# A four-layer graph network: its last two attention layers written as one run of steps

## The chip, the cores and the metric

The kernel runs on one core of a Trainium2 chip. The metric is the device time of one execution in microseconds. The kernel before takes 3355.96 us, the median of 3 runs (3355.28, 3355.96 and 3361.55).

An instruction belongs to one of five engines: TensorE (PE, matrix products; its weight loads are listed apart as PEld), VectorE (DVE), ScalarE (ACT), GpSimd (POOL) and SyncE (SP), which only issues loads. [...] Loads and stores are issued either on SP's queue or on GpSimd's.

## The reference, cut to what matters

Four layers follow one another on N = 2708 nodes of 512 features; each ends in a residual and a layer normalisation. The change touches the last two. `adj` is a 0/1 matrix with ones on the diagonal.

```python
# layer 2
node_att = softmax(x @ node_w, axis=0)
h = x @ edge_w
e = where(adj > 0, h @ h.T, -9e15)
edge_att = softmax(e, axis=1)
x = layernorm(x + (adj * (node_att * edge_att)) @ (x @ weight) + bias)
# layer 3
query, key, value = x @ Wq + bq, x @ Wk + bk, x @ Wv + bv
a = query @ key.T / sqrt(512) + adj + adj
x = layernorm(x + softmax(a, axis=-1) @ value)
```

## The kernel before, in words

**Blocks and groups.** The 2708 rows are cut into 22 blocks (`NT`, line 60): 21 of 128 rows and a last one, block 21, of 20 rows. Layers 2 and 3 treat the query rows in seven groups (`GROUPS`, line 975): six of three blocks, and a last one of blocks 18 to 21 (404 columns). A group's work is a row of 22 score steps, one for each block of keys, and 22 sum steps.

**A score step** (`one_score`, line 1086) loads the 128 x 384 piece of `adj` that belongs to it (`load_a`, five buffers, SP's queue), makes the scores in PSUM (`ps_s`, two banks), masks or biases them into a tile `e`, and takes a running maximum `mx`. Layer 2's scores are symmetric: those that have been made for an earlier group are read back from memory (`load_kept`) and transposed. After its 22nd score step a group spreads its maximum over the partitions (`spread_max`, line 1138). Block 21 has its own path: four partial products in quarters of a bank (L1112), a ScalarE copy, and one product that adds the quarters (L1122).

**A sum step** (`one_sum`, line 1174) subtracts the maximum and takes the exponential, adds to the denominator `acc`, in layer 2 multiplies by `adj` (L1382, with a load of its own), and multiplies by the values (L1195): `sup` in layer 2, `xs` itself in layer 3, where the weight `wv` is applied to the finished sum. Block 21's values come from `values4`, four copies of its 20 rows that GpSimd's queue loads when the layer begins (L1055).

**The end of a group** (`end`, line 1233) takes the denominators (L1245), and puts the work on single blocks into a list `later`. In layer 2 that is `finish2` (line 1384): residual sum (L1388), layer normalisation, and a transpose of the new rows into `hT` (L1003 and L1006), which is then layer 3's key. In layer 3 it is a projection by `wv` (L1273) and `finish3` (line 1438): GpSimd adds bias and residual into `y` (two buffers, L1441), VectorE adds the sum (L1442) and normalises, and GpSimd's queue stores the block (L1446).

**The order.** A loop at line 1290 makes one score step and the sum step that lies `lag` = 25 steps behind, so a layer is 154 + 25 = 179 steps: 25 with scores alone, then 129 with both, then 25 with sums alone. At odd steps of a group one entry of `later` is run; what is left runs after the loop. A scheduler then places each engine's instructions within this order by when they should be ready, so neighbours may be interleaved.

**The two layers** are two calls of `softmax_layer`. Each call opens its own pools of buffers and closes them at its end; between the calls `sup` is freed, and layer 3's weights are loaded into space opened for them: the query weight in four pieces (L1417), `wv` (L1418) and `bv` (L1419). Layer 3's first step makes the query of group 0 (line 1420, products L1013).

Of the kernel before, what the change touches and what calls it, by code (L numbers as in the profile page):

```python
# [29 lines left out]
def gnn_stack_kernel(  # L30
# [991 lines left out]
    def softmax_layer(keys, values, query, score, weigh, finish, after=None, mirror=False):  # L1022
# [5 lines left out]
        AHEAD = 3  # L1028
        HOME = {it: gi for gi, group in enumerate(GROUPS) for it in group}

        def key_order(gi):

            late = list(range(NFULL // 2)) + [NT - 1] + list(range(NFULL // 2, NFULL))
            if not mirror:
                return late
            early = [jt for jt in late if HOME[jt] < gi]
            late = [jt for jt in late if HOME[jt] >= gi]
            place = {jt: (k + 0.5) / len(early) for k, jt in enumerate(early)}
            place |= {jt: (k + 0.5) / len(late) for k, jt in enumerate(late)}
            return sorted(place, key=place.get)  # L1040
# [6 lines left out]
        with (  # L1047
            tc.tile_pool(name="att", bufs=2) as att,
            tc.tile_pool(name="att_ps", bufs=2, space=PSUM) as psum,
        ):  # L1050


            values4 = att.tile([P, F], F32, tag="values4", name="values4", bufs=1)
            for c in range(C):
                nc.gpsimd.dma_start(values4[c * Q : c * Q + REST], values[:REST, NT - 1, :])  # L1055

            def load_a(gi, jt):
                c0, w = GSPAN[gi]
                j0, m = BLOCKS[jt]
                a = att.tile([P, GW], F32, tag="a", name="a_cols", bufs=5)  # L1060
                if m < P:
                    nc.vector.memset(a, 0.0)
                for r in range(0, P, P if m == P else Q):
                    nc.sync.dma_start(a[r : r + m, :w], adjT[j0 : j0 + m, c0 : c0 + w])
                return a

            def load_kept(gi, jt):

                g = HOME[jt]
                src = kept[g, gi][:, j_in(jt)]  # L1070
                s = att.tile([P, GB, P], F32, tag="sm", name="s_kept", bufs=3)
                full = sum(BLOCKS[it][1] == P for it in GROUPS[gi])
                nc.sync.dma_start(
                    s[:, :full, :], src[: full * P].rearrange("(b p) j -> p b j", p=P)
                )
                for b in range(full, len(GROUPS[gi])):
                    n = BLOCKS[GROUPS[gi][b]][1]
                    nc.sync.dma_start(s[:n, b, :], src[b * P : b * P + n])
                return s

            def j_in(jt):

                b = jt - GROUPS[HOME[jt]][0]
                return slice(b * P, b * P + BLOCKS[jt][1])

            def one_score(st, k):
                gi, jt = st["gi"], st["order"][k]
                c0, w = GSPAN[gi]
                j0, m = BLOCKS[jt]
                a = load_a(gi, jt)  # L1090
                ps = psum.tile([P, BANK], F32, tag="ps_s", name="ps_s")
                if mirror and HOME[jt] < gi:
                    s = load_kept(gi, jt)
                    for b, it in enumerate(GROUPS[gi]):
                        n = BLOCKS[it][1]
                        nc.tensor.transpose(
                            ps[:, b * P : b * P + n], s[:n, b, :], ident[:n, :n]
                        )
                elif m == P:
                    for c in range(C):  # L1100
                        nc.tensor.matmul(  # L1101
                            ps[:, :w],
                            keys[:, c, j0 : j0 + P],
                            st["q"][:, c, :],
                            start=(c == 0),
                            stop=(c == C - 1),
                        )
                else:

                    parts = psum.tile([P, BANK], F32, tag="tp", name="ps_parts")  # L1110
                    for c in range(C):
                        nc.tensor.matmul(  # L1112
                            parts[c * Q : (c + 1) * Q, :w],
                            keys[:, c, j0 : j0 + Q],
                            st["q"][:, c, :],
                            start=True,
                            stop=True,
                        )
                e = att.tile([P, GW], F32, tag="e", name="e", bufs=NT + AHEAD + 2)
                if m < P:  # L1120
                    nc.scalar.copy(e[:, :w], parts[:, :w])
                    nc.tensor.matmul(ps[:, :w], quarters, e[:, :w], start=True, stop=True)  # L1122
                if mirror and HOME[jt] > gi:
                    s = att.tile([P, GROUP * P], F32, tag="sraw", name="s_raw", bufs=3)
                    nc.scalar.copy(s[:m, :w], ps[:m, :w])
                    nc.gpsimd.dma_start(kept[gi, HOME[jt]][j_in(jt), :], s[:m, :w])
                score(e[:, :w], ps[:, :w], a[:, :w])
                st["e"].append(e)
                if k == 1:
                    st["mx"] = att.tile([P, GW], F32, tag="mx", name="mx", bufs=1)  # L1130
                    nc.vector.tensor_tensor(
                        st["mx"][:, :w], st["e"][0][:, :w], e[:, :w], ALU.max
                    )
                elif k > 1:
                    mx = st["mx"][:m, :w]
                    nc.vector.tensor_tensor(mx, mx, e[:m, :w], ALU.max)

            def spread_max(st):

                gi = st["gi"]  # L1140
                c0, w = GSPAN[gi]
                k = len(GROUPS[gi])
                tp = psum.tile([P, C, P], F32, tag="tp", name="tp_mx")
                nm = small.tile([P, GB], F32, tag="nm", name="nm")
                dg = att.tile([P, GB, P], F32, tag="dg", name="dg", bufs=1)
                for b, it in enumerate(GROUPS[gi]):
                    n = BLOCKS[it][1]
                    nc.tensor.transpose(
                        tp[:n, b, :], st["mx"][:, b * P : b * P + n], ident
                    )  # L1150
                    nc.vector.tensor_reduce(
                        nm[:n, b : b + 1], tp[:n, b, :], AX.X, ALU.max, negate=True
                    )
                    nc.vector.tensor_scalar(
                        dg[:n, b, :n], ident[:n, :n], nm[:n, b : b + 1], None, ALU.mult
                    )
                pb = psum.tile([P, BANK], F32, tag="tp", name="pb")
                full = sum(BLOCKS[it][1] == P for it in GROUPS[gi])
                nc.tensor.matmul(  # L1159
                    pb[:, : full * P],  # L1160
                    ones,
                    dg[:, :full, :].rearrange("p b i -> p (b i)"),
                    start=True,
                    stop=True,
                )
                for b in range(full, k):
                    n = BLOCKS[GROUPS[gi][b]][1]
                    nc.tensor.matmul(
                        pb[:, b * P : b * P + n], ones[:n], dg[:n, b, :n], start=True, stop=True
                    )  # L1170
                st["nmax"] = att.tile([P, GW], F32, tag="nmax", name="nmax", bufs=2)
                nc.scalar.copy(st["nmax"][:, :w], pb[:, :w])  # L1172

            def one_sum(st, k):
                gi, jt = st["gi"], st["order"][k]
                c0, w = GSPAN[gi]
                j0, m = BLOCKS[jt]
                e = st["e"][k][:, :w]
                nc.vector.tensor_tensor(e, e, st["nmax"][:, :w], ALU.add)
                nc.scalar.activation(e, e, AF.Exp)  # L1180
                if k == 0:
                    st["acc"] = att.tile([P, GW], F32, tag="acc", name="acc", bufs=1)
                    nc.vector.tensor_copy(st["acc"][:, :w], e)
                    st["po"] = [
                        psum.tile([P, F], F32, tag=f"po{(GROUP * gi + b) % C}", name="po", bufs=1)
                        for b in range(C if after is not None else len(GROUPS[gi]))
                    ]
                else:
# [118 lines left out]
            for work in later:  # L1307
                work()
# [211 lines left out]
```

## Time and profile before

| What | Value |
|---|---|
| median of 3 runs | 3355.96 us |
| profiled execution | 3363.59 us |
| its span, first to last instruction | 3361.8 us |
| mean granted TensorE clock | 0.985 of full |
| PE busy | 3272.6 us (97%) |
| VectorE, ScalarE, GpSimd busy | 1991.5, 1344.1, 130.0 us |
| first score product of layer 2 / of layer 3 | 1697.4 / 2410.2 us |
| last product of a sum in layer 2 / in layer 3 | 2387.5 / 3336.2 us |

Times are in us from the first instruction. A row of a timeline gives start, length, engine, line, operation, what it writes and reads by the program's own names, shape and count, and in brackets how long the engine was idle before it and what released it. PE's ends are modelled, since products overlap. Line numbers are those of the kernel before. A float32 product is made in two passes, so a score step of four products shows eight instructions.

### The profile page before, as it was taken

The page shows a single profiled execution, that of the slowest core. Times are in us where ns is not written, and L with a number is a line of the kernel's source. Part 1 is how long each engine was busy: PE and PEld are TensorE (multiplying, and loading weights), DVE is VectorE, ACT ScalarE, POOL GpSimd, SP SyncE. Part 2 cuts the span into 40 slices and gives each one's busy share as a digit, 9 for nine tenths or more (in the row PEclk, how much of TensorE's full clock was granted, in tenths as well). Part 3 has the DMA queues.
Part 4 walks back from the last instruction along what each step waited for, and adds up shares of the span by engine and source line. Part 5 has one row for each costly group of instructions (what it writes and reads, how often), then busy time and mean ns, then how long its engine had stood idle before and what let it go on. Part 6 is the DMA issues. An engine that isn't in the chain of part 4 may idle for free.

```text
span 3361.8 us, 30553 instructions
## 1 busy us (share of the span) xinstructions
PE 3272.6 (97%) x10981; PEld 1751.3 (52%) x10981; DVE 1991.5 (59%) x3228; ACT 1344.1 (40%) x1504; POOL 130.0 (4%) x211
## 2 busy tenths in 40 slices
PE   8999999999999989999999999999999999999998
PEld 5444444544444445886554554444455555555554
DVE  7878967767687585445135666777253442543533
ACT  6888887468877652001133333332011010110110
POOL 1000100000000000000010000000000000000001
PEclk9999999999999999999999999999999999999999
DMA  8746753335534412540044444554211111111100
GB/s 292 249 159 199 274 185 104 112 106 181 183 131 159 157 40 75 140 128 15 0 119 131 118 123 130 141 149 109 63 49 35 44 33 42 37 34 44 35 23 20
DMA packets 168348, 367.32 MB, mean 109 GB/s; under 512 B 20782, under 2 KB 111602, under 8 KB 164804
## 3 DMA queue, kind: packets, MB, share of 16 engines
q1 hardware_dynamic: 153268, 301.55, 30.0%
q0 software_dynamic: 14928, 63.82, 5.0%
q8 instruction: 86, 1.41, 0.2%
q14 instruction: 66, 0.54, 0.1%
HBM read 301.46 MB, written 63.35 MB: 109 GB/s over the span
## 4 chain that ended last, share of the span: by engine, by line
PE 73%; issue 13%; DVE 7%; DMA 3%; ACT 3%; POOL 1%; SPq 0%; POOLq 0%; DVEq 0%; ACTq 0%
PE po L1195 22%; PE ps_s L1101 17%; PE po L397 8%; PE ps_nb L952 7%; PE ps_wide L1013 4%; DVE t L349 3%; PE ps_hid L118 2%; PE ps_sup L1338 2%; PE ps_o L1273 2%; PE ps_mlp L637 2%; DMA a<-adj_d 1%; ACT t L341 1%; DMA a_cols<-in_adjT_dram 1%; PE ps_dec L733 1%; ACT t L350 1%
## 5 line engine op out<-in xcount | busy, mean ns | idle before, releaser
L349 DVE SCALAR_TENSOR_TENSOR t<-t,a 128x2708 f32<-128x2708 f32 (+1 forms) x162 | 480.0, 2974 | 146.6 <-ACT t L341 144.8
L341 ACT ACTIVATE t<-f1b,f2h 128x1354 f32<-128x1354 f32 (+1 forms) x324 | 445.7, 1414 | 93.2 <-PE psm L420 45.1
L397 PE MATMUL po<-t,emb 128*128 128x452 f32 (+3 forms) x1056 | 408.3, 556 | 17.9 <-ACT t L350 10.1
L350 ACT ACTIVATE t<-t 128x2708 f32<-128x2708 f32 (+1 forms) x162 | 396.7, 2452 | 70.3 <-DVE t L349 68.9
L397 PE MATMUL po<-t,xw 128*128 128x452 f32 (+3 forms) x1056 | 415.8, 557 | 9.0 <-ACT ft L499 4.8
L1195 PE MATMUL po<-sup,e 128*128 128x512 f32 x882 | 409.3, 600 | 5.5 <-DVE e L1382 5.5
L1195 PE MATMUL po<-e,xs 128*128 128x384 f32 (+1 forms) x1176 | 407.5, 489 | 0.0
L1101 PE MATMUL ps_s<-q,hT 128*128 128x384 f32 (+1 forms) x1176 | 403.5, 489 | 0.0
L1436 DVE SCALAR_TENSOR_TENSOR e<-a_cols,ps_s 128x384 f32<-128x384 f32 (+1 forms) x154 | 85.6, 556 | 417.3 <-PE ps_s L1101 394.2
L397 PEld LDWEIGHTS po<-t,emb 128*128 128x128 f32 (+1 forms) x1056 | 197.2, 194 | 222.3 <-issue 197.3
L1101 PEld LDWEIGHTS ps_s<-q,hT 128*128 128x128 f32 x1176 | 222.7, 190 | 161.4 <-issue 6.5
L397 PEld LDWEIGHTS po<-t,xw 128*128 128x128 f32 (+1 forms) x1056 | 191.0, 192 | 221.0 <-issue 202.5
L1195 PEld LDWEIGHTS po<-e,xs 128*128 128x128 f32 x1176 | 221.7, 190 | 157.1 <-issue 6.0
L1195 PEld LDWEIGHTS po<-sup,e 128*128 128x128 f32 x882 | 161.8, 191 | 176.5 <-issue 148.4
L1101 PE MATMUL ps_s<-hT 128*128 128x384 f32 (+1 forms) x672 | 229.2, 488 | 1.0 <-ACT sup L1345 0.7
L98 ACT ACTIVATE ln_rstd<-ln_rstd 128x1 f32<-128x1 f32 x88 | 17.2, 201 | 497.5 <-DVE ln_rstd L97 497.0
L1378 ACT ACTIVATE a_cols<-a_cols,neg_big 128x384 f32<-128x384 f32 (+1 forms) x154 | 94.8, 616 | 251.6 <-DMA a_cols<-in_adjT_dram 222.9
L952 PE MATMUL ps_nb<-hid_hi,at 128*128 128x512 f32 x484 | 188.2, 390 | 0.4 <-DVE at L946 0.4
L952 PE MATMUL ps_nb<-hid_lo,at 128*128 128x512 f32 x484 | 187.9, 390 | 0.0
L1172 ACT COPY nmax<-pb 128x384 f32<-128x384 f32 (+1 forms) x14 | 6.7, 478 | 431.2 <-PE pb L1159 350.4
L1101 PEld LDWEIGHTS ps_s<-hT 128*128 128x128 f32 x672 | 125.9, 190 | 97.0 <-issue 19.0
L1190 DVE TENSOR_TENSOR acc<-acc,e 128x384 f32<-128x384 f32 (+2 forms) x294 | 162.6, 553 | 11.2 <-ACT e L1180 1.0
(234 smaller groups left out, 3486.0 us busy)
## 6 DMA issues: line engine op xcount, KB each, us to landing
a<-adj_d SPq DMA_DIRECT2D x116, 677.0 KB
a_cols<-in_adjT_dram SPq DMA_DIRECT2D x378, 192.0 KB
a<-in_adjT_dram SPq DMA_DIRECT2D x42, 677.0 KB
adj_d<-a POOLq DMA_DIRECT2D x42, 677.0 KB, 4.7
raw<-in_adjT_dram SPq DMA_DIRECT2D x105, 256.0 KB
kept<-t POOLq DMA_DIRECT2D x10, 1354.0 KB, 6.4
t<-kept SPq DMA_DIRECT2D x10, 1354.0 KB
a_cols<-in_adjT_dram SPq DMA_DIRECT2D x63, 202.0 KB
```

What stands on the lines that cost most here:

```text
L118: nc.tensor.matmul(ps[:n], xt[:, c, :n], w[:, c, :], start=(c == 0), stop=(c == C - 1))
L341: nc.scalar.activation(tv[:, k, :], f1b[:n, k, :w], AF.Tanh, bias=f2h[:n, jt, h : h + 1], scale=0.5,)
L349: nc.vector.scalar_tensor_tensor(tv, tv, GUARD, ab, ALU.add, ALU.mult)
L350: nc.scalar.activation(tv, tv, AF.Exp, scale=0.5)
L397: nc.tensor.matmul(po[HB * k + q][:, :qw], values[r : r + n, jt, h * P : (h + 1) * P], t[r : r + n, k, q0 : q0 + qw], start=(jt == 0), sto ...
L952: nc.tensor.matmul(pos[it], at, half[:, jt, :], start=(jt == 0 and k == 0), stop=(jt == NT - 1 and k == 1),)
L1013: nc.tensor.matmul(ps[:, :width], w(c, o), xt(c), start=(c == 0), stop=(c == C - 1),)
L1101: nc.tensor.matmul(ps[:, :w], keys[:, c, j0 : j0 + P], st["q"][:, c, :], start=(c == 0), stop=(c == C - 1),)
L1190: nc.vector.tensor_tensor(acc, acc, e[:m], ALU.add)
L1195: nc.tensor.matmul(out, lhsT, rhs, start=(k == 0), stop=(k == NT - 1))
L1378: nc.scalar.activation(a, a, AF.Identity, bias=neg_big[: a.shape[0]], scale=1.0e30)
L1436: nc.vector.scalar_tensor_tensor(e, a, 2.0, ps, ALU.mult, ALU.add)
```

## The change

`softmax_layer` no longer opens pools or loops. It takes the pools and the list `later`, and gives back two functions, one that makes a score step and one that makes a sum step. Both layers share one set of pools, and one loop runs both: 345 steps in place of 179 + 179. Layer 3's query of group 0 and its score steps begin at step 166, while layer 2's sums go on to step 178; its sums begin at step 191.

- Layer 3's tiles that had space of their own now lie in `sup`, in blocks whose last use in layer 2 has gone by: queries in blocks 0 to 7, `wv` in 8 to 11, `bv` in 12, the finished sums in 13 to 16, and `y` in 17 to 20, so that four places take turns instead of two.
- The query weight is loaded at step 154 into buffers that layer 2's stored scores used (three in `sm`, the last quarter in two of `sraw`); `wv` and `bv` are loaded at step 179. All are on SP's queue.
- `values4` is loaded at a layer's first sum step instead of its first step.
- Group 0 of layer 3 takes the key blocks in the order 0 to 21, with block 21 last; the other groups have block 21 in the middle as before.
- Entries of `later` run at odd steps as before, and also at every step that has no sum: layer 2's last four blocks are finished at steps 179 to 182.
- The stores of the last group's four blocks go on SP's queue; those of the other groups stay on GpSimd's.

The diff, cut to its core (the body of the step functions is only indented otherwise):

```diff
+    def softmax_layer(
+        att, psum, later, keys, values, query, score, weigh, finish, after=None, sums=None
+    ):
...
             if not mirror:
-                return late
+                return late if gi else list(range(NT))
...
-            values4 = att.tile([P, F], F32, tag="values4", name="values4", bufs=1)
-            for c in range(C):
-                nc.gpsimd.dma_start(values4[c * Q : c * Q + REST], values[:REST, NT - 1, :])
+        def last_values():
+
+            t = att.tile([P, F], F32, tag="values4", name="values4", bufs=1)
             for c in range(C):
+                nc.gpsimd.dma_start(t[c * Q : c * Q + REST], values[:REST, NT - 1, :])
+            values4.append(t)
...
-                    oT = att.tile([P, C, GW], F32, tag="oT", name="oT", bufs=1)
+                oT = sums()
...
-            later = []
-            states = {}
-            steps = len(GROUPS) * NT
-            lag = NT + AHEAD
-            for t in range(steps + lag):
-                if t < steps:
-                    gi, k = divmod(t, NT)
-                    if k == 0:
-                        states[gi] = {
-                            "gi": gi, "e": [], "q": query(gi, att, psum), "order": key_order(gi)
-                        }
-                    one_score(states[gi], k)
-                    if k == NT - 1:
-                        spread_max(states[gi])
-                if t >= lag:
-                    gi, k = divmod(t - lag, NT)
-                    one_sum(states[gi], k)
-                    if k == NT - 1:
-                        end(states.pop(gi))
-                    elif later and k % 2:
-                        later.pop(0)()
-            for work in later:
-                work()
+        def score_step(t):
+            gi, k = divmod(t, NT)
+            if k == 0:
+                states[gi] = {"gi": gi, "e": [], "q": query(gi), "order": key_order(gi)}
+            one_score(states[gi], k)
+            if k == NT - 1:
+                spread_max(states[gi])
+
+        def sum_step(t):
+            gi, k = divmod(t, NT)
+            if t == 0:
+                last_values()
+            one_sum(states[gi], k)
+            if k == NT - 1:
+                end(states.pop(gi))
+
+        return score_step, sum_step
...
+        def weights3():
+
+            mqk = []
+            for o in range(C):
+                if o + 1 < C:
+                    t = att.tile([P, GB, P], F32, tag="sm", name=f"mqk{o}", bufs=3)
+                    nc.sync.dma_start(t[:, :C, :], mqk_d[o])
...
+        def values3():
+            wv_sb = room(8, 4, C, F)
+            nc.sync.dma_start(wv_sb, wv.rearrange("(c p) o -> p c o", p=P))
+            bv_sb = room(12, 1, F)
+            nc.sync.dma_start(bv_sb, bv.partition_broadcast(P))
...
+        def query(gi):
             c0, w = GSPAN[gi]
-            q = att.tile([P, C, GW], F32, tag="q", name="q")
+            q = room(4 * (gi % 2), 4, C, GW)
...
-            y = att.tile([P, F], F32, tag="y", name="y3")
+            y = room(17 + it % 4, 1, F)
...
-                nc.gpsimd.dma_start(out[i0 : i0 + n, :], y[:n])
+                queue = nc.sync if it in GROUPS[-1] else nc.gpsimd
+                queue.dma_start(out[i0 : i0 + n, :], y[:n])
...
+        steps = len(GROUPS) * NT
+        lag = NT + AHEAD
+        start3 = steps + 12
+        assert start3 + GROUPS[-1][0] >= steps + lag + GB
+        for t in range(start3 + steps + lag):
+            if t == steps:
+                weights3()
+            if t == steps + lag:
+                values3()
+            if t < steps:
+                score2(t)
+            elif 0 <= t - start3 < steps:
+                score3(t - start3)
+            k = None
+            for first, step in ((lag, sum2), (start3 + lag, sum3)):
+                if 0 <= t - first < steps:
+                    step(t - first)
+                    k = (t - first) % NT
+            if later and (k is None or (k % 2 and k < NT - 1)):
+                later.pop(0)()
+        for work in later:
+            work()
```

`room(first, blocks, *shape)` is a view of `blocks` blocks of `sup` from block `first` on.

## The prediction

> **What bounds the kernel now.** I read the table of stretches first, cutting the run at the layer boundary and at the end. Columns: length, then busy time (and instructions) of TensorE (PE), its weight loads, VectorE (DVE), ScalarE (ACT), GpSimd (POOL); then granted PE clock, DMA share, GB/s.
>
> ```profile
> 2330.00:2389.85 59.85, 59.84 (x175) 23.57 (x173) 21.68 (x50) 10.70 (x18) 0.00 (x0) 1.00 0.17 42
> 2389.85:2399.76 9.91, 3.26 (x17) 2.61 (x17) 7.67 (x26) 2.74 (x9) 1.40 (x2) 0.66 0.93 329
> 2399.76:2483.00 83.24, 79.84 (x247) 46.01 (x247) 35.84 (x72) 11.80 (x23) 3.27 (x5) 0.98 0.21 54
> 2483.00:3280.00 797.00, 796.96 (x2508) 453.36 (x2507) 336.48 (x699) 97.85 (x209) 27.21 (x30) 1.00 0.14 37
> 3336.70:3361.80 25.10, 14.77 (x41) 5.82 (x39) 11.50 (x29) 0.81 (x4) 4.63 (x6) 0.86 0.09 33
> ```
>
> Layer 2's last sums keep PE busy 59.84 of 59.85 us, and layer 3's body 796.96 of 797. A change of order can gain nothing there: the same matmuls remain. What can be gained lies in rows two and five, and 3.4 us in row three.
>
> The timeline of PE shows what row two consists of (start, length; idle time before and its releaser in brackets), under a steady example from layer 2:
>
> ```profile
> 2340.51 0.60 PE L1003 MATMUL tp<-ident,xs 128*128 128x128 f32 x4
> ...
> 2396.05 3.26 PE L1003 MATMUL tp<-ident,xs 128*128 128x128 f32 x16 [6.21 <-DVE xs L113]
> 2399.76 10.59 PE L1013 MATMUL ps_wide<-hT,mqk 128*128 128x384 f32 x32 [0.45 <-ACT hT L1006]
> ```
>
> After the last product, four blocks are finished on VectorE while TensorE waits 6.21 us; the 16 transposes then take 3.26 us, another 0.45 us goes by, and only then does layer 3's first query start. In the chain of waits a steady set of four transposes takes 0.44 us, so 16 are worth 1.76.
>
> Last, the end. The timeline of VectorE and GpSimd, and the rows of the closing line:
>
> ```profile
> 3350.93 1.26 POOL L1441 TENSOR_TENSOR y<-xs,bv_sb 20x512 f32<-20x512 f32 x1 [1.81 <-DMA out_dram<-y]
> 3352.22 0.74 DVE L1442 SCALAR_TENSOR_TENSOR y<-ps_o,rs,y 20x512 f32<-20x512 f32 x1 [1.15 <-POOL y L1441]
> 3355.34 0.52 POOL L1446 DMA_DIRECT2D out_dram<-y  x1 [2.66 <-DVE y L113]
> ...
> L1516 POOLq DRAIN x3: 46/99/5683, 3355.3 to 3361.5; - x3
> L1516 SPq DRAIN x3: 7/7/7, 3357.7 to 3361.3; - x3
> L1516 PEldq DRAIN x2: 13/3058/6103, 3345.4 to 3361.3; - x2
> ```
>
> PE is done at 3345.4 + 6.1 = 3351.5, yet the last block's sum starts at 3352.22, because GpSimd's addition into y had to wait for a store to free one of two y buffers. SyncE (SP), which waits for every store, passes at 3357.7. GpSimd's DRAIN begins as its last store is issued, at 3355.3, and takes 5.68 us, to 3361.0; the closing barrier ends the span 0.8 us later. GpSimd's drain sets the end, not the landing.
>
> **The boundary.** The change puts layer 3's query and scores 0 to 12 beside layer 2's last 13 sum steps. A score step costs PE 2.58 us (32 matmuls in 10.32 us, four steps), one of these sum steps (10.50 + 1.00) / 4 = 2.87. Side by side they make 5.45 per step, no less than one after the other: nothing is gained in the overlap itself. The gain is row two: when the last sum ends, scores 13 to 17 are ready to run, 5 × 2.58 = 12.9 us that need no late block. At best 9.91 − 1.76 = 8.15 us goes.
>
> What is late next? VectorE must close four blocks and serve those scores. From 2389.00 it took 7.0 us to the first transpose; two or three scores in that time add 1.1 us each (scores' e and running maximum, 0.55 + 0.56), so some 10 us if shared. PE's cover is 0.9 us of small matmuls plus 12.9, so score 18, the first that needs a late block, is not late. The order of instructions can still hurt: the program lists the first transposes right after score 13, which PE reaches at 0.9 + 2.6 = 3.5 us, while that block's chain alone (first three sums 2.5, score 13's two operations 1.1, the fourth sum 0.9, normalisation 2.2) takes 6.7: 3.2 us of idle PE. But the other 18 blocks of layer 2 are listed in the same way, each behind its own normalisation, and the waits list has 7.3 us for this wait in all, 6.2 of it here: 1.1 us over the rest. Instructions are plainly interleaved with ready work (the steady transposes stand between products). Bounds of what remains: 0 and 4.9 (below); I take 0.8, nearest to the steady rows. **Gain 7.3 us.**
>
> A rule bears on the upper bound. Row: after 6.21 us idle the clock granted from 2392 to 2398 is 0.50 to 0.52, and the transposes need 0.21 us each instead of 0.11; after 3.93 us idle at a group's end (2317) it is 0.53 for 3 us; after layer 3's broken idle at 2468 (1.24 us at most in one piece) row three still has 0.98. The Trainium skill, "TensorE: Matmul & The Clock Gate", Part 1, halves the clock after an idle window of about 3.4 us and asks as much busy time to restore it; the window runs freely. By the rule a remaining 3.2 us wait can cost half of 3.4 us more, 1.7, so 4.9; by the rows a wait near 1 us costs only itself. I go by the rows for the value, by the rule for the bound. The rule also says that the saved clock loss is no extra gain: it is already inside the 3.26.
>
> **Hidden parts of the move.** The overlapped steps ask VectorE for five operations, 2.8 us, of 5.45, and the loads for two tiles per step, as in all of layer 2: nothing. Layer 3's first set of sums has its usual lag. Its group 0 now takes block 21 last, not in the middle: its 0.60 us wait for the ScalarE copy moves and keeps its price, and the 2.8 us of idle at the first spread of the maximum (1.24 + 0.39 + 0.38 + 0.80) stay, since no sums run there. So row three's 3.4 us is not gained.
>
> **Loads.** Five query-weight loads now stand in SP's queue at the last score of layer 2, and wait there until the transposes of blocks 15 to 17 free their buffers, at 2304.1 on the old clock; loads for layer 2's sums are queued behind. Issue: 5 × 0.43 = 2.2 us. The cover: SP's last load before the group's end was issued at 2304.94, the next at 2320.86, as VectorE needs nothing new before 2320. Cost nothing; without that cover, 2 us of issue plus 3 us for 1 MB at 329 GB/s. wv (1 MB) and bv stand before score 13's loads: 3 us against five loaded tiles ahead, 5 × 2.58: nothing. GpSimd's four small loads of the last value rows move from each layer's start to its first sum: 4 × 0.51 us, used ten or more steps later: nothing; their lateness would cost at most their 4.3 us.
>
> **The end.** With four y places, block 21's addition runs early, after block 17's store lands (issued 3298.2 + 2.6). Its sum then starts at 3351.55 instead of 3352.22, 0.7 us sooner, and its normalisation (2.8 us) ends at 3354.35. The store goes by SP. No store on SP is in the trace: its landing is bounded by the 1.9 us of 40 KB loads on GpSimd's queue and the 2.6 us median of 256 KB stores; below, 1.5, if the 0.5 us issue there is mostly saved. I take 1.9, same size: 3356.3, and with 0.8 for the barrier 3357.1, against 3361.8: 4.7, of which I count 4.6 (3.9 to 5.1). GpSimd's drain now begins near 3303, 48 us of cover for its 5.7; with that cover gone the gain would be the 0.7.
>
> Here two rules speak against so much. "DMA: Bandwidth & Descriptors", Specifications, has a first byte at 1 us by GpSimd and 0.6 by SP: 0.4 gained. "VectorE: DVE Perf Modes", The DRAIN you can't avoid, calls the drains at a program's ends about 12 ns on all engines: then no drain is saved, and 0.7 + 0.4 = 1.1 is all. The row has 5683 ns. I go by the row. **Gain 4.6 us.**
>
> **Sum.** 7.3 + 4.6 = 11.9 us. Span 3361.8 → 3349.9; the profiled execution, 3363.59, would become 3351.7. It lies 7.6 us above the median of the runs, which I take off alike: 3355.96 − 11.9 = 3344.1.
>
> **Rivals.**
> - *Both gains as summed*: 3344.1, own range 3341 to 3347. Chance 0.64.
> - *The wait moves into the transposes*: 3.2 us idle behind score 13 plus 1.7 of clock; the boundary gives 3.2, total 7.8: 3348.2. For it: VectorE is nearly full for 10 us. Against: 1.1 us over 18 blocks. Chance 0.21.
> - *The overlap doesn't happen* (layer 3's query or scores wait for something of layer 2's last sums): only the end gains, 3351.4. For it: query results go into the space of values still in use. Against: the query's four blocks are read in the first eight steps of that group, before it starts. Chance 0.10.
> - *Slower: one big tile, ordered as a whole.* Queries, sums, weights and outputs of layer 3 all lie in sup. If accesses to one tile were ordered whatever part they touch, each output block's chain (3344.59 to 3347.5, 2.9 us) would stand before the next score that reads the query. 18 blocks × 2.9 = 52 us: 3396. It decides from 11.9 / 2.9, over four such waits. Against: hT is one tile also, ScalarE writes its blocks while scores read others, and the list of waits has no score waiting for that. Chance 0.05.
>
> **The numbers.** A measurement can tell about 0.2% from no change, 6.7 us: faster means below 3349.2. The first case is; of the second about 0.16, by the spread of its bounds; the third is "same" with the rest. Faster 0.80, same 0.15, slower 0.05. Low end: both gains in full, 13.2 us, and 0.1% for the medians (the three runs before span 6.3 us): 3339.5. High end: the second case and 2 us: 3350.5; the last two are left out, 0.15.
>
> **What would show it.** Right: no PE idle over 1 us at the boundary, transposes in fours between scores at 0.11 us each, clock 1.0 throughout; SP's last store near 3354 on the old clock less 7, GpSimd's drain long before. Wrong: a wait for DVE xs before the first transposes with the clock at 0.5; a long GpSimd drain at the end still; PE waits in the body of layer 3, now 0.04 us; or loads late in the overlapped steps.

## The result and the profile after

The changed kernel takes 3348.45 us, the median of 9 runs (3344.59 to 3354.89), against 3359.08 for the kernel before in 9 runs (3355.28 to 3366.54). The ratio is 0.9969, 95% interval 0.9961 to 0.9978: some 10.4 us (7 to 13) faster. The forecast was a gain of 11.9 us, to 3344.1 us; of the 4.3 us between that and 3348.45, 3.1 lie in the kernel before, which took 3355.96 us in the first 3 runs and 3359.08 in all 9.

The profiled spans differ by more, 3361.8 to 3346.3, and 4.0 us of that is no effect of the change: layer 2's first score product starts at 1697.45 before and at 1693.43 after, though nothing ahead of it was edited. In the traces of this study that start lies anywhere from 1692.7 to 1700.2 (1693.2 in the kernel before with one line moved at its very end). So the two traces, and all experiments, are compared from there on, in two pieces:

| Piece | before | after | difference | forecast |
|---|---|---|---|---|
| first score product of layer 2 to last sum product of layer 3 ("the middle") | 1638.8 | 1631.6 | -7.2 | -7.3 |
| last sum product to the end of the span ("the end piece") | 25.6 | 21.3 | -4.3 | -4.6 |

A single trace can carry such differences: kernels whose instructions up to the last sum product are the same have middles of 1638.8 and 1639.0 us (the kernel before, twice) and of 1631.6, 1631.6 and 1631.7 (the changed kernel, three times). The end piece with the stores on SP's queue varies more, from 20.9 to 21.5 us.

**The boundary.** The table of stretches of the changed kernel, in the columns of before, cut in the overlapped steps, around the end of layer 2's last sum, around layer 3's first spread of the maximum, and in the body of layer 3:

```profile
2363.00:2425.00 62.00, 62.00 (x184) 30.34 (x183) 18.70 (x32) 0.00 (x0) 3.75 (x3) 1.00 0.30 86
2425.00:2445.00 20.00, 20.00 (x77) 10.88 (x76) 13.57 (x43) 4.43 (x10) 3.50 (x5) 1.00 0.21 52
2445.00:2470.00 25.00, 21.51 (x65) 11.55 (x64) 15.20 (x34) 8.13 (x17) 0.00 (x0) 0.86 0.16 42
2470.00:3270.00 800.00, 799.96 (x2517) 454.93 (x2517) 338.21 (x707) 100.08 (x213) 27.64 (x30) 1.00 0.14 36
```

The second row is the boundary: TensorE is busy for 20.00 of 20.00 us at full clock, where it had been idle for 6.66. The timeline of TensorE shows by what:

```profile
2427.71 0.97 PE L1252 MATMUL pr<-ones,acc 128*128 128x1 f32 x8
2428.61 0.91 PE L1108 MATMUL ps_s<-sup,hT 128*128 128x384 f32 x2
2429.45 1.03 PE L1268 MATMUL ps_po<-po,quarters 128*20 128x512 f32 x2
2430.41 8.01 PE L1108 MATMUL ps_s<-sup,hT 128*128 128x384 f32 x24
2438.26 0.60 PE L1003 MATMUL tp<-ident,xs 128*128 128x128 f32 x4
```

The closing of the last group (pr, ps_po) is followed at once by scores (ps_s), 26 passes of them, a little more than three score steps, before the first transposes. Those come after 9.6 us, when VectorE has closed the first block, and no bracket shows a wait. They were not put right behind score 13, as the program lists them.

**The end.** The timeline of VectorE and SP, and the rows of the closing line (durations in ns, least, median and most, then the first and the last start):

```profile
3332.85 10.64 SPq L1484 DMA_DIRECT2D out_dram<-sup  x4
3340.33 0.74 DVE L1479 SCALAR_TENSOR_TENSOR sup<-ps_o,rs,sup 20x512 f32<-20x512 f32 x1 [0.63 <-PE ps_o L1280]
...
L1593 POOLq DRAIN x3: 46/99/6120, 3289.4 to 3346.0; - x3
L1593 SPq DRAIN x3: 7/7/7, 3345.4 to 3345.7; - x3
```

The last block's sum is released by TensorE itself (ps_o), no longer by GpSimd. GpSimd's long drain begins at 3289.4, 57 us before the end. SP's last store is issued at 3343.19, SP passes at 3345.4, the span ends at 3346.3.

### The profile page after: what moved, and what is told of

Same layout as the page of the kernel before. It is cut to its first block, busy times and chain, and to the rows that moved or that the text cites. A ratio compares the mean times of both kernels' runs of the same rounds, so it can differ in the third digit from the quotient of the medians.

```text
span 3346.3 us, 30537 instructions
## 1 busy us (share of the span) xinstructions
PE 3268.7 (98%) x10981; PEld 1747.0 (52%) x10981; DVE 1991.2 (60%) x3228; ACT 1344.2 (40%) x1504; POOL 128.7 (4%) x207
## 4 chain that ended last, share of the span: by engine, by line
PE 75%; issue 12%; DVE 6%; ACT 3%; DMA 3%; POOL 1%; SPq 0%; POOLq 0%; DVEq 0%; ACTq 0%
PE po L1202 22%; PE ps_s L1108 17%; PE po L397 10%; PE ps_nb L952 7%; PE ps_wide L1013 4%; PE ps_hid L118 2%; PE ps_sup L1339 2%; PE ps_o L1280 2%; PE ps_dec L733 2%; DVE t L349 2%; PE ps_mlp L637 1%; ACT t L341 1%; DMA a_cols<-in_adjT_dram 1%; ACT t L350 1%; DMA a<-adj_d 1%
## 5 line engine op out<-in xcount | busy, mean ns | idle before, releaser
L1108 PE MATMUL ps_s<-sup,hT 128*128 128x384 f32 (+1 forms) x1176 | 406.9, 490 | 0.0
L1108 PEld LDWEIGHTS ps_s<-sup,hT 128*128 128x128 f32 x1176 | 222.0, 190 | 164.1 <-issue 14.1
```

What stands on the lines that cost most here:

```text
L1108: nc.tensor.matmul(ps[:, :w], keys[:, c, j0 : j0 + P], st["q"][:, c, :], start=(c == 0), stop=(c == C - 1),)
```

## The experiments

Theory: the gain is (1) work that stands ready on TensorE behind layer 2's last sum, and (2) at the end, GpSimd's drain that no longer comes last. Rivals: the overlapped steps gain in themselves; the queue gains only by a shorter landing. Experiments that ran once are read from their traces by the two pieces. Line numbers in a fence are those of its own kernel.

### The end piece: which part of it gains

Stores back on GpSimd's queue:

```diff
-                queue = nc.sync if it in GROUPS[-1] else nc.gpsimd
+                queue = nc.gpsimd
```

> The changed kernel with one line undone: the last group's four stores go on GpSimd's queue again; the four y places stay. Measured by the end piece, from the start of the last sum product to the end of the span: 25.6 us before, 21.3 after. Theory 1 (GpSimd's drain of about 5 us begins when its last store is issued and sets the end): the last store is issued near 18.3 us into the piece, the drain ends 5.7 later, the barrier adds 0.75: 24.9 us. Theory 2 (only the landing differs by queue, 0.4 us): 21.7 us. The part of the run before it is unchanged: first score product to last sum product 1631.6 us.

Measured: end piece 25.0 us, middle 1631.7. The closing line's rows:

```profile
L1593 POOLq DRAIN x3: 46/106/5677, 3345.4 to 3351.5; - x3
L1593 SPq DRAIN x3: 7/7/124, 3347.7 to 3351.6; - x3
```

SP knows all stores landed at 3347.7, but GpSimd drains from 3345.4 to 3351.1. Theory 1 had 24.9, the rival 21.7. The four y places alone are thus worth 25.6 - 25.0 = 0.6 us.

Only the stores moved, in the kernel before:

```diff
-                nc.gpsimd.dma_start(out[i0 : i0 + n, :], y[:n])
+                queue = nc.sync if it in GROUPS[-1] else nc.gpsimd
+                queue.dma_start(out[i0 : i0 + n, :], y[:n])
```

> The kernel before with one line of the change: the last group's four stores on SP's queue; y keeps two buffers. Theory 1: the last block's addition still waits for block 19's store to land (0.7 us late or a little less), and GpSimd's drain begins only when that addition ends, near 16 us of the end piece: it would be over near 21 and the store lands near 21.0 too, so the end piece is 21.9 us against 25.6 (22.0 if the drain is last). Theory 2 (queue's landing alone): 25.2 us. First score to last sum product as before, 1638.7 us.

Measured: end piece 21.3 us, middle 1639.0.

```profile
3345.83 1.25 POOL L1441 TENSOR_TENSOR y<-xs,bv_sb 20x512 f32<-20x512 f32 x1 [2.44 <-DVE ln_rstd L97]
...
L1517 POOLq DRAIN x3: 46/106/6104, 3345.8 to 3353.2; - x3
L1517 SPq DRAIN x3: 7/7/7, 3352.7 to 3353.0; - x3
```

The one line gives the whole gain of the end, 4.3 us. My 21.9 was too high: the last addition starts 13.7 us into the piece in place of 14.7 (3350.93 before), so that with the stores on SP the last block's sum is not late any more even with two y buffers. The drain, from 3345.8 to 3351.9, is over before SP passes at 3352.7. The two parts are worth 4.3 and 0.6 apart, and 4.3 together.

Is it the store, or any late work on GpSimd? A small copy was added behind the last block, into space that nothing reads any more:

```diff
                 queue.dma_start(out[i0 : i0 + n, :], y[:n])
+                if it == NT - 1:
+                    nc.gpsimd.tensor_copy(room(0, 1, F)[:n, :8], y[:n, :8])
```

> The changed kernel, stores of the last group on SP as in it, with one small GpSimd copy (20 x 8) added that reads the last normalised block, so that GpSimd has work, but no store, at the very end. If any late GpSimd work brings a drain of about 4.9 us: the copy starts at 18.1 us of the end piece, takes some 0.3, the drain ends at 23.3, with the barrier 24.0 us. If the long drain belongs to a store just issued on that queue: 21.3 to 21.5 us.

Measured: 24.1 us. The timeline of GpSimd has the copy at 18.3 us of the piece, and the closing line the drain:

```profile
3346.93 0.18 POOL L1486 COPY sup<-sup 20x8 f32<-20x8 f32 x1 [52.68 <-DVE sup L113]
```

```profile
L1595 POOLq DRAIN x3: 46/106/5021, 3346.9 to 3352.5; - x3
```

A copy of 0.18 us costs 2.8 us at the end of the span (24.1 against 21.3). So my theory was too narrow: not the last *store* on GpSimd starts the long drain, but its last *work*, whatever it is. What the change does at the end is to take GpSimd's last work away from there.

### The boundary: overlap, or ready work

No overlap, but the same shared buffers:

```diff
-        start3 = steps + 12
+        start3 = steps + 25
```

> The changed kernel with layer 3 starting at step 179 in place of 166 (358 steps): no score of layer 3 stands beside a sum of layer 2, but pools and list are still shared, so query and scores 0 to 17 are ready when the last sum ends. Theory 1 (the gain is ready work behind the last sum, the side-by-side steps are worth nothing): first score product to last sum product stays at 1631.6, within 0.7 us. Theory 2 (the early start itself gains): it goes back towards 1638.7, by half or more.

Measured: middle 1634.8 us, between the two: 3.2 of the 7.2 us were lost. Timeline of TensorE, then the stretch behind it:

```profile
2385.02 0.97 PE L1252 MATMUL pr<-ones,acc 128*128 128x1 f32 x8
2385.85 1.02 PE L1268 MATMUL ps_po<-po,quarters 128*20 128x512 f32 x2
2388.71 12.28 PE L1013 MATMUL ps_wide<-hT,mqk 128*128 128x384 f32 x32 [1.84 <-DVE rs L1262]
```

```profile
2389.22:2392.64 3.42, 3.42 (x7) 1.85 (x6) 3.20 (x14) 0.00 (x0) 0.00 (x0) 0.50 0.00 0
```

The query was ready, but its first product waited 1.84 us for VectorE to read a denominator (rs, L1262): pr and ps_po hold both PSUM buffers of the tag `tp`, and the query needs one. Behind the wait the clock is 0.50 for 3.42 us, all of it busy, 1.7 lost: 3.5 us, about the 3.2 that are missing. Two runs separate this from the overlap. First, a start at step 176, so that the query and three scores have gone by:

```diff
-        start3 = steps + 12
+        start3 = steps + 22
```

> The changed kernel with layer 3 starting at step 176: its query and three scores stand before the end of the last sum, not thirteen. In the run without any overlap the first query product waited 1.84 us for a PSUM buffer of the two that the closing of the last group also uses, and the clock then halved. Theory 1b (what counts is ready work that needs none of those two buffers, that is scores; how many steps overlap is worth nothing): first score to last sum product 1631.6, within 0.6 us. Theory 2 (each overlapped step gains): 3 of 13 steps, so of the 3.2 us between 1634.8 and 1631.6 about 0.7: 1634.1 us.

Measured: 1631.2 us. Three overlapped steps do as much as thirteen, to within 0.4 us: that much more lies between layer 2's last group end and layer 3's first sum than in the changed kernel, and 0.8 us less in layer 2, ahead of any step of layer 3 (the table under "Why the prediction was right"). Second, no overlap at all, but with the closing's two PSUM tiles taken from the idle score banks (both new lines stand in `end`):

```diff
-            pr = psum.tile([P, BANK], F32, tag="tp", name="pr")
+            free = "ps_s" if mirror and NT - 1 in GROUPS[gi] else "tp"
+            pr = psum.tile([P, BANK], F32, tag=free, name="pr")
...
-                    ps = psum.tile([P, F], F32, tag="tp", name="ps_po4")
+                    ps = psum.tile([P, F], F32, tag=free, name="ps_po4")
```

> The run without overlap (start at step 179), with the two PSUM tiles of layer 2's last closing (pr and ps_po4) taken from the two score banks, which are idle there, so that the query's products find both of their buffers free. If these buffers are the whole of what the run without overlap lost: the 1.84 us wait ahead of the first query product goes, and with it the half clock behind it (3.4 us, 1.7 lost): first score to last sum product 1631.5 us, as in the changed kernel, with no step of the layers side by side. If the overlapped steps matter in themselves: 1634 to 1635 us still.

Measured: 1631.6 us. The timeline of TensorE has no wait:

```profile
2389.71 0.91 PE L1013 MATMUL ps_wide<-hT,mqk 128*128 128x384 f32 x2
2390.55 1.03 PE L1269 MATMUL ps_po<-po,quarters 128*20 128x512 f32 x2
2391.51 9.94 PE L1013 MATMUL ps_wide<-hT,mqk 128*128 128x384 f32 x30
```

Without one step of overlap the whole gain of the boundary is there (in the table, 143.0 us in both). The overlap is worth nothing in itself; ready work with free PSUM buffers is worth all of it.

### The order of key blocks in layer 3's first group

The forecast gave block 21's move to the end no price. The traces show one place where after is worse than before: the clock at the first spread of the maximum. Two runs tried to take it back. Start at step 176, with

```diff
-                return late if gi else list(range(NT))
+                return late
```

> As the run with the start at step 176, but group 0 of layer 3 takes block 21 as its eleventh key block, as in the kernel before (its rows are ready in time from this start). If putting block 21 last is what brought the 0.6 us wait next to the waits of the spread maximum and halved the clock some 3 us longer: 1.0 us less than the run with block 21 last, 1630.6, with the clock at 1.0 until the spread has ended as before. If the order is worth nothing: 1631.6.

Measured: 1631.1 us against 1631.2. The half-clock stretch at the first spread is 6.83 us long in both, and nothing was gained. And the changed kernel with

```diff
-                return late if gi else list(range(NT))
+                return late if gi else list(range(18)) + [21, 18, 19, 20]
```

> The changed kernel (start at step 166) with group 0 of layer 3 taking block 21 as its 19th key block, three score steps (7.7 us) ahead of the spread maximum. By the same theory 1630.6 us from first score to last sum product; if the order is worth nothing 1631.6.

Measured: 1633.1 us, 1.5 *more* than the change. Here the clock did what the theory says: the stretch is 3.41 us long in place of 6.83, and up to layer 3's first sum product the run is 0.7 us ahead of the changed kernel. But layer 3's sums then take 2.2 us more (844.8 us for 842.6), for a reason that has nothing to do with the clock. Timeline of TensorE in this run:

```profile
2574.06 0.91 PE L1202 MATMUL po<-e,values 20*128 20x384 f32 x4
2575.37 0.33 PE L1155 MATMUL tp_mx<-ident,mx 128*128 128x128 f32 x1 [0.40 <-DVE mx L1143]
2575.63 0.91 PE L1202 MATMUL po<-e,values 20*128 20x384 f32 x2
...
2576.72 0.91 PE L1202 MATMUL po<-e,values 20*128 20x384 f32 x2
```

and the same products in the changed kernel:

```profile
2601.45 0.93 PE L1202 MATMUL po<-e,values 20*128 20x384 f32 x8
```

Block 21's four products use 20 rows of the array each, in four quarters, and run side by side: eight passes in 0.93 us, about what two passes take alone (0.91). In 19th place its sum step meets the next group's spread, whose transposes are put between them: the eight passes take three times 0.91 us, and TensorE waits 0.40 us for a transpose's input, together the 2.2 us.

### A further step

The changed kernel still waits 3.93 us at the end of group 5 of layer 2, and the list of waits of that stretch names VectorE's multiplication by adj:

```profile
PE po L1202 <- DVE e L1392: 3.9, 1, 3.9
```

The single buffer of the denominator could be what holds it:

```diff
-                st["acc"] = att.tile([P, GW], F32, tag="acc", name="acc", bufs=1)
+                st["acc"] = att.tile([P, GW], F32, tag="acc", name="acc", bufs=2)
```

> The run with block 21 as 19th key block, with two buffers for the denominator acc in place of one. At a layer 2 group's end the next group's first acc copy, and behind it the multiplication by adj that TensorE waits for, waits until the old acc has been read: 3.93 us of idle TensorE at 2316 us and half clock for 3 us after it (1.5 us). If the buffer is what holds the multiplication: up to 5.4 us less, 1625.2 us from first score to last sum product. If VectorE's order holds it (the three sums of the ending group stand first): no change, 1630.6.

Measured: 1622.1 us, 11.0 less than the same kernel with one buffer; twice what was expected, because other groups' ends had lost time in the same way. Layer 2 takes 12.7 us less: 4.1 at the end at 2316 us, 5.4 at the one at 2231, and 3.2 ahead of them. A half-clock stretch in layer 3, at 2564.67 us, which the run with one buffer does not have, takes 1.7 back. Alone on the changed kernel, and with the start at 176 and block 21 in the middle:

> The changed kernel with two acc buffers and nothing else. The run with two acc buffers and block 21 in 19th place had 1622.1 us from first score to last sum product against 1633.1 with one. Its order of group 0 cost about 2 us, so this one: 1620.5, span 3335 to 3338, ratio to the kernel before about 0.9935 (0.9969 from the change and 11 us more). If block 21's place was not the cost: 1622.

> Start at step 176, block 21 as eleventh key block in all groups of layer 3, two acc buffers. By the theory that neither the number of overlapped steps nor the order matters: the same as the changed kernel with two acc buffers, 1620.5 us from first score to last sum product, within 1 us, which the half-clock windows can shift; ratio to the kernel before about 0.9935.

Measured: middle 1620.3 and 1618.1 us. The second lies 2.4 us under its expectation: 1.3 us at layer 3's first spread, where its half-clock stretch is 3.41 us long and that of the first 6.83, and 0.9 in layer 2. Times: 3335.98 us (ratio 0.9930, interval 0.9916 to 0.9943) and 3333.07 us (0.9922, 0.9909 to 0.9934) against 3360.79 for the kernel before in the same session; the intervals of the two overlap. Both beat the changed kernel's 0.9969. The timeline of TensorE of the first, at the place of the 3.93 us:

```profile
2304.80 5.40 PE L1202 MATMUL po<-sup,e 128*128 128x512 f32 x12
...
2312.01 0.63 PE L1003 MATMUL tp<-ident,xs 128*128 128x128 f32 x4 [0.75 <-DVE ln_rstd L99]
```

The products of the next group (po) run on; what is left is a wait of 0.75 us for a normalisation.

## Why the prediction was right

The middle can be cut once more, at two products that every trace has: the 801st product `po<-sup,e` of layer 2's sums (2343.53 us before, 2339.38 after), which comes after all half-clock stretches of layer 2's own group ends and ahead of any step of layer 3, and layer 3's first sum product (2493.64 and 2482.40).

| Run | layer 2 up to the 801st product | from there to layer 3's first sum | layer 3's sums |
|---|---|---|---|
| before | 646.1 | 150.1 | 842.6 |
| before, stores on SP | 646.2 | 150.2 | 842.6 |
| after | 645.9 | 143.0 | 842.6 |
| no overlap | 645.8 | 146.4 | 842.6 |
| no overlap, free banks | 646.0 | 143.0 | 842.6 |
| start at 176 | 645.1 | 143.5 | 842.6 |
| start at 176, block 21 in the middle | 645.0 | 143.5 | 842.6 |
| block 21 19th | 646.0 | 142.4 | 844.8 |
| two acc, block 21 19th | 633.2 | 142.3 | 846.5 |
| two acc | 634.1 | 143.7 | 842.6 |
| two acc, start at 176, block 21 in the middle | 633.1 | 142.4 | 842.6 |

All of the change's gain in the middle, 7.1 us, lies in the second column.

What it consists of is shown by two more tables: idle TensorE, and the busy time at half clock, half of which is lost. Before (the whole middle, then each stretch in which the granted clock was 0.50):

```profile
1697.45:3336.23 1638.78, 1617.23 (x5009) 870.64 (x5009) 829.54 (x1796) 352.81 (x693) 76.94 (x115) 0.99 0.27 75
2238.47:2241.88 3.41, 3.41 (x5) 1.33 (x4) 2.50 (x6) 0.75 (x2) 0.00 (x0) 0.50 0.79 238
2320.39:2323.80 3.41, 2.91 (x4) 1.35 (x5) 3.41 (x10) 0.20 (x1) 0.00 (x0) 0.50 0.35 77
2392.07:2398.90 6.83, 2.85 (x13) 2.30 (x13) 5.45 (x22) 1.87 (x6) 0.54 (x1) 0.50 0.96 331
2470.57:2473.99 3.42, 3.38 (x6) 1.90 (x7) 1.21 (x3) 1.71 (x2) 0.00 (x0) 0.50 0.00 0
```

After:

```profile
1693.43:3325.03 1631.60, 1617.73 (x5009) 870.27 (x5010) 830.07 (x1796) 353.15 (x693) 79.89 (x117) 0.99 0.27 76
2231.04:2237.87 6.83, 6.06 (x10) 2.53 (x10) 4.89 (x12) 0.81 (x2) 0.00 (x0) 0.50 0.66 185
2316.38:2319.79 3.41, 3.19 (x4) 1.51 (x5) 3.41 (x10) 0.20 (x1) 0.00 (x0) 0.50 0.37 87
2456.32:2463.15 6.83, 5.26 (x10) 2.75 (x10) 3.74 (x11) 2.28 (x3) 0.00 (x0) 0.50 0.10 29
```

Idle: 1638.78 - 1617.23 = 21.6 before, 13.9 after. Lost to the half clock: (3.41 + 2.91 + 2.85 + 3.38) / 2 = 6.3 before, (6.06 + 3.19 + 5.26) / 2 = 7.3 after. What remains is 1610.9 and 1610.5, the same work. So idle fell by 7.7 and the clock's loss rose by 1.0: it fell by 1.4 at the boundary, and rose by 1.3 at 2231, 0.1 at 2316 and 0.9 at the first spread.

- *Row two is the gain, the overlap none*: right. The 6.66 us of idle and the third half-clock stretch (1.4 us lost) are gone, 8.1 us in all, and the run without overlap but with free banks has the same 1631.6 us.
- *0.8 us of wait remains at the transposes* (bounds 0 and 4.9): 0.0 measured, so the boundary gave 8.1 of the 8.15 us that the prediction had called the best case. The steady rows were the right guide; the bound by the clock's rule did not come into play there. In the run without overlap it did, and sooner than the rule that the prediction cites has it: a wait of 1.84 us, not 3.4, and 1.7 us lost to the clock behind it. There the measurement decides, not the rule.
- *Block 21 last "keeps its price"*: wrong, it cost about 1.0 us, of which 0.9 by the clock. The forecast read row three's mean of 0.98 as no loss of clock at the first spread, and took from it that a wait near 1 us costs only itself; in fact that mean is the stretch from 2470.57 to 2473.99 at half clock. After the change the pieces of idle stand together (0.60, 1.32, 0.39, 0.39, 0.80 in 5.7 us) and the stretch is twice as long: (5.26 - 3.38) / 2 = 0.9. In all seven traces with block 21 last it is 6.83 us, in five of six others 3.41. The sixth, with block 21 in the middle and the start at 176, has 6.83 too, which is why moving it gave nothing there. So the order favours the longer stretch, but does not decide it. What goes with the length in all thirteen traces is how far ahead of the stretch the longest of these waits (1.24 to 1.33 us) began: 1.5 to 3.1 us for 6.83, 3.75 to 4.9 for 3.41. How much of that is the order and how much chance was not separated.
- *Luck*: the 0.8 us of wait that did not come and the 1.0 us at the first spread that was not forecast cancel. That the middle was met to 0.1 us (7.2 for 7.3) is luck; the mechanism of the larger term is right.
- The rise at 2231 is no effect of the change: of the ten traces with one acc buffer seven had 6.83 us there and three 3.41, and the kernel before had 3.41 in its own trace and 6.83 in the one with the stores on SP, with the same instructions up to there. Nor is it a loss to the change: layer 2 up to the 801st product takes 646.1 us before and 645.9 after, as the longer stretch goes with less idle time (over the middle 20.3 us in the kernel before with the stores on SP, 21.6 in its own trace). So the two sums above are an account of where time stands, and not of what each stretch costs.
- *The end*: 4.3 us for 4.6. The last sum started 0.7 us sooner, as forecast; SP's landing took 2.2 us (issued at 3343.19, last passed at 3345.4) where 1.9 was taken. The other traces with these stores on SP have 1.9 to 2.3, so the missing 0.3 us is within what varies. The drain went by row and not by rule, which was right: by the two rules that the prediction cites the end would have gained 1.1.
- *Loads*: right. In the boundary and in the overlapped steps TensorE is busy throughout (62.00 of 62.00 and 20.00 of 20.00), so no load was late for it.
- *One big tile*: 799.96 busy of 800 us in layer 3's body. The work on parts of sup shows no wait for one another.

The 11.5 us of the two pieces and the 10.4 of the ratio agree within the interval. The time alone would not have told the first rival from the second, whose gain of 7.8 us lies in the interval of 7 to 13 too, and whose 3348.2 us is nearer to the measured median; the traces do, since the second has a wait ahead of the first transposes, and there is none.

## What to carry to other kernels

At a seam between two stages of a kernel bound by one engine, ask what that engine can do while the last results are being closed, and whether the buffers for it are free of the closing; work that can start there at once was worth the whole gain here, and the steps side by side nothing. Look at the closing rows of each engine: the last work on GpSimd should be early, as a drain of some 5 us followed it in every trace here. Where a result moves by a few microseconds, take apart idle time and half-clock time before giving a cause to either, and compare from a point behind the code that was not touched. The same product in both traces is the safer mark: idle time and half clock can trade against each other without any change in the time.

## What the runs showed of the hardware that was not expected

- GpSimd's closing drain ends about 5 us after its last work, store or not: it takes 5.68 us with the 0.5 us issue of a store in it, 5.02 with a 0.18 us copy in it, and 6.12 with a 1.26 us addition in it.
- In layers 2 and 3 the half clock came in stretches of 3.41 or 6.83 us only. In each trace all of them begin on one grid of 3.413 us (after: 2231.04, 2316.38 and 2456.32, which are 25 and 41 such lengths apart), and where a wait falls on it goes with its price: the same wait of 1.86 us near 2231 was followed by 6.83 us in the seven traces where it began 1.0 to 1.8 us ahead of the stretch, and by 3.41 us in the three where it began 1.9 to 3.6 us ahead. The half clock was also granted after idle pieces of which none was longer than 1.33 us, at the first spread of layer 3, in every trace.
- Four products of 20 rows each ran side by side where they followed each other without others between, eight passes in 0.93 us; broken up by transposes into three, they took 0.91 us three times.
- VectorE's last scaling of a block (L113, 0.55 us alone) took 1.32 us in the kernel before at 3346.94, while GpSimd's addition ran from 3346.73 to 3347.98, and 0.81 and 1.07 us beside such additions in that kernel with the stores on SP. No experiment separates the two.
